# A two-layer LoRA and attention kernel on one core: unit 3's heads transposed on TensorE, the first matrix in three pieces, layer 0's results turned by blocks and an exchange

## The chip, the cores and the metric

The kernel runs on one NeuronCore of a Trainium2 chip. The core has a matrix engine (TensorE, PE in the profile; its weight loads are PEld), a vector engine (VectorE, DVE), a scalar engine (ScalarE, ACT), a general engine (GpSimd, POOL), and a sequencer that mostly issues transfers (SyncE, SP). 16 DMA engines move data between HBM and the on-chip memory. Each engine runs its own list of instructions in order and waits on semaphores for the others.

The metric is the device time of the whole kernel in microseconds. Before the change it is 1206.94 us, the median of three runs (1206.44 to 1207.21).

## What is computed

Eight sequences (B = 8) of 128 rows by 512 columns, all in float32, go through two layers. Each layer adds its result to its input.

```python
# layer 0, per sequence b
c   = x[b] @ weight[adapter_ids[b]].T               # 512 x 512, an adapter's own matrix
w   = softmax over the best 2 of 8 gates (c @ gate_w.T)
x1  = x[b] + c @ base_w.T + base_b + 2 * sum_e w[e] * (c @ A[e].T) @ B[e].T
# layer 1, per sequence b
q, k, v = x1 @ Wq.T, x1 @ Wk.T, x1 @ Wv.T           # 32 query heads, 8 key heads of 128
q, k    = rope(rmsnorm(q)), rope(rmsnorm(k))
o       = attention(q over 512 cached rows from 16 pages, plus the 128 own rows)
y       = o @ Wo.T
out     = x1 + 2 * (gates of 64 small experts * (y @ A_w.T)) @ B_w.T
```

## The kernel before

**Order of the work.** The order is written out by hand for all five engines: each engine's instructions run in the order in which the code emits them. Data dependences are kept by semaphores; a tile that reuses a buffer waits for the last reader of the buffer's former tile.

**Layer 0** is a loop of eight steps, `t = 0..7`. TensorE at step t does: `l0_adapter(t)` in two halves (the adapter's matrix times `x`, 16 products in 32 matmul instructions), between them `l0_turn_low(t - 1)` (a transpose of the gated low-rank values), then `l0_turn(t - 2)`, then `l0_experts(t - 1)` (L686, which completes the layer's result), then `l0_base(t)` (gates and base matrix, L640 and L645). From step 4 on pieces of layer 1 for units 0 and 1 stand in between: `project_whole` (L295), `norms`, `rotate`, `transpose_qk` and, at steps 6 and 7, the scores of unit 0.

`l0_experts(b)` makes the result `x1` on VectorE (L688), stores it to HBM, finds a power of two that brings it to range, and scales it on ScalarE into the buffer `xb` (L696). Layer 1's projections need that result with columns across the partitions. `l0_turn(b)` does this: four transposes of 128 by 128 on TensorE (L705) into a PSUM bank, and a copy by ScalarE (L707) into a half of `xo`. `xo` has four pairs of sequences with seven places each; places 0 to 3 hold the two results of a pair, 4 to 6 later hold sums.

Ahead of the loop TensorE runs `WARM` = 20 transposes of the identity matrix (L727). The first adapter matrix comes in two transfers of 512 KB, the others in one of 1 MB. SP issues these loads (`l0_load`), the loads of `x` (`l0_load_x`; three `xb` buffers, so the load for b + 3 waits until `l0_turn(b)` has read the buffer), the gathers of key pages and the stores of results, all in one queue. POOL issues the loads of projection weights (`load_q`).

**Layer 1** works in 64 units: a unit is one of the eight key heads of one sequence, with its four query heads. `iteration(u)` does, for unit u, four scores (`scores`, L436 for the cached keys and L439 for the own rows) into the two alternating PSUM banks `s0` and `s1`, masking with the smallest value taken along (`mask_exp`, VectorE L449), the exponential (ScalarE L460), the division by the sum (POOL L466), and for earlier units the values (`values(u - 2)`, L953) and the output projection.

The probabilities must be transposed before the values. This is done in two steps: VectorE transposes blocks of 32 by 32 into the tile `pb` (`blocks`, L471), and an exchange through HBM moves the blocks across partitions: `exchange_out(u)` writes `pb` to `px` with four transfers (L483, two each by SP and ScalarE's queue), `exchange_in(u)` reads it back as `pT` in the next iteration (L933). There is one `pb` buffer.

The rotated heads of unit u + 2 (four query heads and the key head) ride in the same exchange: `blocks_qk(u + 2, u)` transposes them by blocks into the rear columns of `pb` (L422), `exchange_in` reads them back as `qkb` (L930), and `heads_qk` copies them to `qkT` on ScalarE (L940). This holds for units 3 to 63. The heads of units 0, 1 and 2 are transposed on TensorE by `transpose_qk` (L361) and copied from PSUM (L366). Unit 0's `pb` lies in a free part of the weight tile `wo_t`.

At the end of the kernel six of the last layer's gated rows are transposed in a similar way by helpers that the change uses too: `turn_blocks` (VectorE, L372), `turn_out` (four writes to HBM, L380), `turn_in` (one read, L387), `turn_chunks` (a ScalarE copy that puts the blocks in order, L393).

`homes` is a tile of five places for the attention's outputs; the first is written by `evict_o(0)` in iteration 3.

Of the kernel before, what the change touches and what calls it, by code (L numbers as in the profile page):

```python
# [16 lines left out]
P = 128  # L17
B = 8
S = 128
DM = 512  # L20
# [18 lines left out]
SCALE = D ** -0.5  # L39
E1, R1, RD = 64, 8, 16  # L40
SC1 = 2.0
WARM = 20
TINY = 2.0 ** -60
EXPONENT = 0x7F800000
BIG = 3.0e38
# [13 lines left out]
def adaln_ffn_kernel(  # L59
# [98 lines left out]
    def sums_q(eng, g, *tees):  # L158

        w = wq_t[g]  # L160
        for t in tees:
            to, x, y = {3: (5, 3, 1), 2: (4, 5, 0), 4: (6, 2, 4), 1: (1, 1, 0)}[t]
            eng.tensor_tensor(w[:, to], w[:, x], w[:, y], ALU.add if t == 2 else ALU.subtract)  # L163
# [207 lines left out]
    def turn_blocks(rows, room):  # L371
        nc.vector.transpose(  # L372
            room.rearrange("p (k c a) -> p c k a", k=QD, c=NC),
            rows.rearrange("p (c k a) -> p c k a", c=NC, k=QD),
        )
# [10 lines left out]
    def turn_in(m, room):  # L386
        nc.sync.dma_start(  # L387
            out=room.rearrange("p (i f) -> p i f", i=QD), in_=m.rearrange("k b i f -> (k b) i f")
        )

    def turn_chunks(out, room):

        nc.scalar.copy(  # L393
            out.rearrange("p c (i a) -> p c i a", a=32),
            room.rearrange("p (i c a) -> p c i a", i=QD, c=NC),
        )
# [15 lines left out]
    def new_pb(u):  # L412

        if u == 0:
            home = wo_t[:, :4].rearrange("p x n -> p (x n)")[:, : QD * PW]
            pb_t[u] = home.rearrange("p (i f) -> p i f", i=QD)
            return
        pb_t[u] = wk1.tile([P, QD, XW], F32, tag="pb", name=f"pb_{u}")

# [56 lines left out]
    def exchange_out(u):  # L476

        pb = pb_t.pop(u)
        m = dram_x.tile([QD, 32, QD, XW], F32, tag="px", name=f"px_{u}")
        w = XW if u + 2 in range(3, NU) else PW  # L480
        for i in range(QD):
            eng = nc.sync if i < QD // 2 else nc.scalar
            eng.dma_start(  # L483
                out=m[:, :, i, :w].rearrange("k b f -> b k f"),
                in_=pb[i * 32 : (i + 1) * 32, :, :w],
            )
        px_t[u] = m


    with ExitStack() as l0:  # L490
# [6 lines left out]
        def l0_load(b):  # L497
            xT = p2.tile([P, NC, S], F32, tag="xT", name=f"xT_{b}", bufs=3)
            eng = nc.scalar if b == 0 else nc.sync
            eng.dma_start(out=xT.rearrange("p c n -> p (c n)"), in_=xt[b])  # L500
            wt = wt_home.pop(b)
            a = nc.sync.value_load(ids[0:1, b : b + 1])
            at = range(0, DM + 1, 2 * P if b == 0 else DM)
            for n, end in zip(at, at[1:]):
                nc.sync.dma_start(
                    out=wt.rearrange("p o n -> p (o n)")[:, NC * n : NC * end],
                    in_=w0[ds(a, 1), :, NC * n : NC * end].rearrange("e p n -> p (e n)"),
                )
            loaded[b] = [xT, wt]

        def l0_load_x(b):
            xb = p2.tile([P, DM], F32, tag="xb", name=f"xb_{b}", bufs=3)
            nc.sync.dma_start(out=xb, in_=x[b])
            loaded[b].append(xb)
# [169 lines left out]
        def l0_experts(b):  # L684
# [13 lines left out]
            nc.gpsimd.tensor_scalar(eps[:, b : b + 1], s, s, EPS, ALU.mult, ALU.mult)  # L698
            state[b] = xb

        def l0_turn(b):
            x1 = state.pop(b)
            tp = bank("o" if b >= B - 2 else "q", f"x1tp_{b}")
            for c in range(NC):
                nc.tensor.transpose(tp[:, c * S : (c + 1) * S], x1[:, c * P : (c + 1) * P], ident)  # L705
            half = xo[:, b // 2, b % 2 * 2 : b % 2 * 2 + 2]
            nc.scalar.copy(half.rearrange("p x c s -> p (x c s)"), tp[:, :DM])  # L707
# [20 lines left out]
        for t in range(B):  # L728
            l0_adapter(t, True)
            if t >= 1:  # L730
                l0_turn_low(t - 1)
            if t == 7:
                scores(0, 1, 1)
                mask_exp(0, 1)
                normalize(0, 0)
            l0_adapter(t, False)
            if t == 0:
                l0_fold()
            if t + 3 < B:
                l0_load(t + 3)  # L740
            if t + 2 < B:
                l0_load_x(t + 2)
            if t in (3, 4):
                load_q(t - 3)
            if 2 <= t <= 5:
                gather(0, (t - 2) * 4, (t - 1) * 4)
            elif t > 5:
                gather(1, (t - 6) * 8, (t - 5) * 8)
            if t >= 2:
                l0_turn(t - 2)  # L750
            if t == 4:
                project_whole(0, 0, 0, 1)
            if t == 5:
                norms(0)
                make_mask(0)
                project_whole(0, 1, 0, 1)
            if t == 6:
                transpose_qk(0)
                project_whole(0, 0, 1, 1)
            if t == 7:  # L760
                make_tables(2)
                norms(2)
                project_whole(0, 1, 1, 1)
                transpose_qk(1)
            if t >= 1:
                l0_experts(t - 1)
            if t == 7:
                scores(0, 2, 1)
                mask_exp(0, 2)
                normalize(0, 1)  # L770
                new_pb(0)
                blocks(0, 0)
            l0_base(t)
            if t == 0:
                l0_small()
            if t == 1:
                l0_rows()
                nc.vector.tensor_scalar_mul(nw[:, 0, :], nw[:, 0, :], -SCALE)
            if 1 <= t <= 4:
                l0_angles(t - 1)  # L780
            if t in (3, 6):
                gather_v(t // 3 - 1, 0, LC)
            if t in (4, 5):
                make_tables(t - 4)
            if t == 4:
                project_whole(0, 0, 0, 0)
            if t == 5:
                project_whole(0, 1, 0, 0)
                norms(1)
                rotate(0)  # L790
                sums_q(nc.gpsimd, 0, 3, 2)
            if t == 6:
                scores(0, 0, 1)
                mask_exp(0, 0)
                project_whole(0, 0, 1, 0)
                rotate(1)
                sums_q(nc.gpsimd, 0, 4)
            if t == 7:
                scores(0, 3, 1)
                mask_exp(0, 3)  # L800
                normalize(0, 2)
                blocks(0, 1)
                project_whole(0, 1, 1, 0, "kv")
# [8 lines left out]
        blocks(0, 2)  # L812
        blocks(0, 3)
        exchange_out(0)
        l0_turn(B - 2)
        l0_experts(B - 1)
        scores(1, 1)
# [104 lines left out]
    with ExitStack() as l1:  # L922
# [2 lines left out]

        def exchange_in(u):
            m = px_t.pop(u).rearrange("k b i f -> (k b) i f")
            if u + 2 in range(3, NU):
                qkb = wk1.tile([P, QD, NH * 32], F32, tag="qkb", name=f"qkb_{u + 2}")
                nc.sync.dma_start(out=qkb, in_=m[:, :, PW:])  # L930
                qkb_t[u + 2] = qkb
            pT = wk1.tile([P, QD, PW], F32, tag=f"pT{u % 2}", name=f"pT_{u}")
            nc.sync.dma_start(out=pT, in_=m[:, :, :PW])  # L933
            pT_t[u] = pT
# [325 lines left out]
        def iteration(u):  # L1260
# [48 lines left out]
            for h in range(REP):  # L1309
                if on(u):  # L1310
                    if (u, h) not in ((1, 0), (1, 1), (2, 0)):
                        scores(u, h)
                        mask_exp(u, h)
                    if h > 0 and (u, h) != (1, 1):
                        normalize(u, h - 1)

                    sums_o(u, h)
                    sums_w(u, h)
                    if 16 <= u < NU - 8 and (r, h) == (2, 3):
                        load_o(u // 16, (1, B12))  # L1320

                    if h == 2:
                        new_pb(u)
                        if u + 2 in range(3, NU):
                            blocks_qk(u + 2, u)
                    if h > 1:
                        blocks(u, h - 2)
                    if h == 1 and u == NU - 5:
                        f_fold()
                    if h == 3:  # L1330
                        z_blocks(u - NU + 4)
                    if h == (1 if u == NU - 3 else 2) and fb is not None:
                        yT_t[fb] = f_turn(fb, *f)
                if on(u - 3):
                    output(u - 3, h)
                    sums_a(u - 3, h)
                if h > 0 and slots:
                    project(k, j, slots[h - 1 : h])

                if (u, h) in WHOLE:  # L1340
                    project_whole(1, *WHOLE[u, h])
            if on(u - 3):
                add_output(u - 3, False)
            if on(u + 1) and (u + 1) % GH == 0:
                make_mask(units[u + 1][0])
            if u + 1 in range(3, NU):
                heads_qk(u + 1)

            if u < NU - 8:
# [202 lines left out]
```

## Time and profile before

| | |
|---|---|
| median of three runs | 1206.94 us (1206.44 to 1207.21) |
| the profiled execution | 1206.82 us |
| its span, first to last instruction | 1205.1 us |
| TensorE matmul busy | 1193.9 us, 99% |
| VectorE, POOL, ScalarE busy | 913.4, 741.0, 504.1 us |
| moved by DMA | 302.97 MB, mean 251 GB/s |
| layer 0's loop | from 6.9 us to about 109 us of the span |
| unit 3's first scores | at 145.81 us |

The busy shares are over the whole span. A matmul's duration overlaps with the next one's; what a group costs TensorE is the distance from its start to the next group's start. The timeline gives for each entry its start, its duration (or the sum of a merged group), the engine, the line, the operation, the tiles written and read, and in brackets the idle time before it with what ended it. The windows view gives the busy time of each engine in a stretch, the clock that TensorE was granted there (1.00 is full speed) and the DMA engines' share and rate. The chain of waits follows the work that ended last back through what released it.

### The profile page before, as it was taken

What the parts mean: (1) busy time and instruction counts of PE and PEld (TensorE: products, weight loads), DVE (VectorE), ACT (ScalarE), POOL (GpSimd) and SP (SyncE); (2) the same over time, 40 slices, a digit from 0 to 9 for tenths busy, and PEclk for the clock granted to TensorE, in tenths of its full rate; (3) what the DMA queues carried; (4) which work ended last, traced back from release to release, by engine and by line L of the source; (5) the groups of instructions that cost most, each with busy time, mean ns of one, the idle gap of its engine ahead of it and who ended that gap; (6) DMA issues with size and microseconds to landing.
All of it is one profiled execution on the core that took longest, in us unless ns stands there. A gap on an engine that the chain in (4) does not pass through costs nothing.

```text
span 1205.1 us, 16763 instructions
## 1 busy us (share of the span) xinstructions
PE 1193.9 (99%) x4147; PEld 716.3 (59%) x4147; DVE 913.4 (76%) x2104; ACT 504.1 (42%) x1457; POOL 741.0 (61%) x828
## 2 busy tenths in 40 slices
PE   9999999999999999999999999999999999999998
PEld 7666455565555556555556565555656565565554
DVE  2547788788888787878888887889887888887632
ACT  1345544444444443444444444444444444443211
POOL 3545769778755587578757685787657684643100
PEclk9999999999999999999999999999999999999999
DMA  8823787888878988898789878987889887897742
GB/s 317 290 85 113 243 249 237 266 279 274 264 253 256 304 242 262 270 297 290 246 252 289 292 230 283 299 287 246 270 256 298 256 262 246 270 286 228 234 137 99
DMA packets 205684, 302.97 MB, mean 251 GB/s; under 512 B 84755, under 2 KB 119828, under 8 KB 204564
## 3 DMA queue, kind: packets, MB, share of 16 engines
q1 hardware_dynamic: 170692, 197.30, 53.4%
q10 hardware_dynamic: 18576, 52.21, 13.6%
q0 software_dynamic: 16320, 52.40, 12.4%
q8 instruction: 33, 0.54, 0.2%
q14 instruction: 63, 0.52, 0.1%
HBM read 185.77 MB, written 116.06 MB: 250 GB/s over the span
## 4 chain that ended last, share of the span: by engine, by line
PE 89%; DMA 4%; DVE 2%; POOL 2%; issue 1%; SPq 1%; ACT 1%; ACTq 0%; DVEq 0%; POOLq 0%
PE o L953 20%; PE p L262 19%; PE s L436 17%; PE y L1078 13%; PE s L439 4%; PE p L295 3%; DMA px<-pb 3%; PE cp L623 2%; PE y L1091 2%; PE op L1439 2%; PE bp L645 2%; PE fr L863 1%; DVE pb L471 1%; PE fz L863 1%; DMA kt<-in_kc 1%
## 5 line engine op out<-in xcount | busy, mean ns | idle before, releaser
L460 ACT ACTIVATE p<-p,low 128x640 f32<-128x640 f32 x256 | 211.8, 827 | 432.8 <-DVE den L465 269.6
L466 POOL TENSOR_SCALAR p<-p,den 128x640 f32<-128x640 f32 x256 | 209.8, 820 | 228.3 <-DVE den L465 227.2
L449 DVE CUSTOM_DVE_ANT_0 p<-s,mask,rs 128x640 f32<-128x640 f32 x256 | 222.3, 879 | 80.8 <-PE s L439 80.2
L262 PE MATMUL p<-wqkv,xo 128*128 128x384 f32 x784 | 280.5, 486 | 0.0
L436 PE MATMUL s<-kt,qkT 128*128 128x512 f32 x504 | 258.2, 594 | 5.3 <-ACT qkT L940 2.9
L953 PE MATMUL o<-pT,vt 128*128 128x512 f32 x512 | 230.2, 592 | 0.0
L471 DVE STREAM_TRANSPOSE pb<-p 128x640 f32<-128x640 f32 x252 | 207.9, 826 | 19.9 <-POOL p L466 19.8
L1078 PE MATMUL y<-wo,oT 128*128 128x256 f32 x784 | 206.4, 380 | 0.0
L262 PEld LDWEIGHTS p<-wqkv,xo 128*128 128x128 f32 x784 | 148.5, 190 | 68.2 <-POOL wqkv L163 0.5
L439 PEld LDWEIGHTS s<-qkT 128*128 128x128 f32 x504 | 95.8, 190 | 120.5 <-issue 120.5
L203 POOL DMA_INDIRECT vt<-in_vc,vrow x128 | 138.5, 1082 | 41.7 <-issue 31.3
L953 PEld LDWEIGHTS o<-pT,vt 128*128 128x128 f32 x512 | 97.2, 190 | 107.9 <-issue 92.5
L436 PEld LDWEIGHTS s<-kt,qkT 128*128 128x128 f32 x504 | 94.7, 190 | 77.4 <-issue 28.9
L1078 PEld LDWEIGHTS y<-wo,oT 128*128 128x128 f32 x784 | 131.9, 191 | 8.6
L311 ACT ACTIVATE sq<-c 128x128 f32<-128x128 f32 x320 | 98.9, 309 | 9.5 <-DVE pb L471 1.4
L439 PE MATMUL s<-qkT 128*128 128x128 f32 x504 | 96.8, 274 | 0.0
L317 POOL TENSOR_TENSOR rs<-ss,mhalf 128x5 f32<-128x5 f32 x64 | 82.4, 1288 | 5.3
L976 ACT COPY oT<-o 128x512 f32<-128x512 f32 x64 | 37.4, 585 | 102.2 <-PE o L953 88.2
L315 POOL TENSOR_SCALAR ss<-ss,eps 128x5 f32<-128x5 f32 x64 | 27.5, 429 | 75.6 <-ACT sq L311 75.6
L422 DVE STREAM_TRANSPOSE pb<-ca 128x640 f32<-128x640 f32 x61 | 50.9, 834 | 19.8 <-DMA px<-pb 10.6
L953 PE MATMUL o<-pT,vn 128*128 128x512 f32 x128 | 65.4, 592 | 0.0
L265 DVE TENSOR_TENSOR c<-c,p 128x384 f32<-128x384 f32 x84 | 44.8, 534 | 24.2 <-PE p L262 23.9
(197 smaller groups left out, 1442.1 us busy)
## 6 DMA issues: line engine op xcount, KB each, us to landing
pT<-px SPq DMA_DIRECT2D x64, 1280.0 KB, 7.5
px<-pb SPq DMA_DIRECT2D x122, 400.0 KB, 5.5
px<-pb ACTq DMA_DIRECT2D x122, 400.0 KB, 5.5
qkb<-px SPq DMA_DIRECT2D x61, 320.0 KB, 3.5
kt<-in_kc SPq DMA_DIRECT2D x512, 32.0 KB, 4.7
wqkv<-in_wqkv POOLq DMA_DIRECT2D x32, 384.0 KB, 4.9
wo<-in_wo POOLq DMA_DIRECT2D x17, 512.0 KB, 7.6
yd<-yp POOLq DMA_DIRECT2D x12, 512.0 KB, 9.4
```

The source lines that it names most:

```text
L203: nc.gpsimd.indirect_dma_start(out=kv_t[step][1][:, c, :], out_offset=None, in_=vc, in_offset=bass.IndirectOffsetOnAxis(ap=vrow[:, hf, at ...
L262: nc.tensor.matmul(out=ps, lhsT=xo[:, pr, x, c, :], rhs=w[:, c, :], start=(c == 0), stop=(c == 1))
L311: nc.scalar.activation(sq, cs[:, at : at + D], AF.Square, accum_out=ss[:, h : h + 1])
L317: nc.gpsimd.tensor_tensor(rs, ss, mhalf, ALU.pow)
L436: nc.tensor.matmul(out=s[:, :L], lhsT=qkT[:, h, :], rhs=kt[:, :, g % GH, :], start=True, stop=True)
L439: nc.tensor.matmul(out=s[:, L:NK], lhsT=qkT[:, h, :], rhs=qkT[:, REP, :], start=True, stop=True)
L449: nc.vector.tensor_tensor_reduce(out=p, in0=s_t.pop((u, h))[:, :NK], in1=mask_t[st], scale=rs_t[u][:, h : h + 1], scalar=BIG, op0=ALU.add, ...
L460: nc.scalar.activation(p, p, AF.Exp, bias=low, scale=-1.0, accum_out=den)
L466: nc.gpsimd.tensor_scalar(p_t[u, h], p_t[u, h], den, 1.0, ALU.mult, ALU.mult)
L471: nc.vector.transpose(pb_t[u][:, :, h * w : (h + 1) * w].rearrange("p i (j a) -> p j i a", a=32), p_t.pop((u, h)).rearrange("p (j i a) -> ...
L953: nc.tensor.matmul(out=o, lhsT=vt[:, c, j * D : (j + 1) * D] if c < LC else vn_t.pop(u), rhs=pT[:, c], start=(c == 0), stop=(c == LC),)
L1078: nc.tensor.matmul(out=y_t["y"][:, half * HN : (half + 1) * HN], lhsT=part(key)[:, i * S : (i + 1) * S], rhs=wo_t[:, slot(w, key[0] // (B ...
```

## The change

- `WARM` becomes 24.
- The first adapter matrix comes in three transfers, of 256, 256 and 512 KB.
- The results 0 to 5 of layer 0 are no longer transposed on TensorE. At the end of step t (1 to 6) `l0_out(t - 1)` turns the result by blocks on VectorE into a room in `xo` and writes it to HBM with four transfers of SP; in the middle of the next step `l0_in` reads it back; at the step after that `turn_chunks` copies it into its half on ScalarE (for result 5 after the loop). Results 6 and 7 stay on TensorE. `l0_load_x(t + 2)` moves on SP's queue from ahead of the gathers to the end of the step, after `l0_out`.
- Unit 3's heads no longer ride in unit 1's exchange. `transpose_qk(3)` does them on TensorE in iteration 1, after the scores of head 2; it takes one turn of the two score banks. The exchange of unit 1 is that much smaller (320 instead of 400 KB a transfer).
- Unit 1's blocks go to the tile `homes` instead of the `pb` buffer.

```diff
-WARM = 20
+WARM = 24
...
+    def x1_room(b):
+        return xo[:, (0, 1, 3)[b % 3], 4:6].rearrange("p x c s -> p (x c s)")
+
+    def x1_half(b):
+        return xo[:, b // 2, b % 2 * 2 : b % 2 * 2 + 2].rearrange("p x c s -> p (x c) s")
...
         if u == 0:
             home = wo_t[:, :4].rearrange("p x n -> p (x n)")[:, : QD * PW]
             pb_t[u] = home.rearrange("p (i f) -> p i f", i=QD)
+            return
+        if u == 1:
+            pb_t[u] = homes.rearrange("p x n -> p (x n)").rearrange("p (i f) -> p i f", i=QD)
             return
...
-        w = XW if u + 2 in range(3, NU) else PW
+        w = XW if u + 2 in range(4, NU) else PW
...
-            at = range(0, DM + 1, 2 * P if b == 0 else DM)
+            at = (0, P, 2 * P, DM) if b == 0 else (0, DM)
...
+        def l0_out(b):
+            room = x1_room(b)
+            turn_blocks(state.pop(b), room)
+            x1m_t[b] = turn_out(f"x{b}", room)
+
+        def l0_in(b):
+            turn_in(x1m_t.pop(b), x1_room(b))
...
             if t + 3 < B:
                 l0_load(t + 3)
-            if t + 2 < B:
-                l0_load_x(t + 2)
...
-            if t >= 2:
-                l0_turn(t - 2)
             if t == 4:
                 project_whole(0, 0, 0, 1)
...
+            if t >= 3:
+                turn_chunks(x1_half(t - 3), x1_room(t - 3))
+            if t >= 2:
+                l0_in(t - 2)
             if t >= 1:
                 l0_experts(t - 1)
...
+            if 1 <= t < B - 1:
+                l0_out(t - 1)
+            if t + 2 < B:
+                l0_load_x(t + 2)
...
         exchange_out(0)
+        turn_chunks(x1_half(B - 3), x1_room(B - 3))
         l0_turn(B - 2)
...
-            if u + 2 in range(3, NU):
+            if u + 2 in range(4, NU):
                 qkb = wk1.tile([P, QD, NH * 32], F32, tag="qkb", name=f"qkb_{u + 2}")
...
+                    if (u, h) == (1, 2):
+                        transpose_qk(3)
+
                     sums_o(u, h)
...
-                        if u + 2 in range(3, NU):
+                        if u + 2 in range(4, NU):
                             blocks_qk(u + 2, u)
...
-            if u + 1 in range(3, NU):
+            if u + 1 in range(4, NU):
                 heads_qk(u + 1)
```

More of the change, by code (lines that the diff above doesn't have):

```diff
@@ L699, in l0_experts @@
             state[b] = xb
+        x1m_t = {}
+        def l0_out(b):
[4 more added lines that the diff above has]
+            turn_in(x1m_t.pop(b), x1_room(b))
         def l0_turn(b):
```

## The prediction

> **What bounds the kernel now.** I read the page's busy times first, then the gaps in TensorE's timeline, then the granted clock around the largest gap, then the chain of waits through it, and last the rows of operations that already do what the change adds.
>
> The page:
>
> ```profile
> PE 1193.9 (99%) x4147; PEld 716.3 (59%) x4147; DVE 913.4 (76%) x2104; ACT 504.1 (42%) x1457; POOL 741.0 (61%) x828
> ```
>
> TensorE is the bound: work taken from it counts, work moved to other engines counts only where TensorE then waits for it. Its timeline (start, duration, what, idle before it):
>
> ```profile
> 1.36 4.53 PE L727 MATMUL idle<-ident 128*128 128x128 f32 x20 [1.36 <-POOL ident masks.py:199]
> 6.92 5.60 PE L623 MATMUL cp<-xT,wqkv 128*128 128x128 f32 x32 [1.03 <-DMA wqkv<-in_w]
> ...
> 30.61 0.60 PE L705 MATMUL x1tp<-ident,xb 128*128 128x128 f32 x4
> 31.05 1.02 PE L686 MATMUL bp<-lb,lowT 128*128 128x512 f32 x2
> ...
> 98.51 0.71 PE L361 MATMUL tq<-ident,ca 128*128 128x128 f32 x5
> 99.05 1.02 PE L686 MATMUL bp<-lb,lowT 128*128 128x512 f32 x2
> ...
> 141.93 1.02 PE L953 MATMUL o<-pT,vn 128*128 128x512 f32 x2
> 145.81 1.12 PE L436 MATMUL s<-kt,qkT 128*128 128x512 f32 x2 [2.85 <-ACT qkT L940]
> ```
>
> Matmuls overlap, so a group's price is start to next start: four transposes of a layer-0 result 0.44 us (30.61 to 31.05), five head transposes 0.54 us (98.51 to 99.05). Only two idle stretches are over 1 us: 1.03 us ahead of the first real matmul, and 2.85 us ahead of unit 3's first scores. The second costs twice. Windows around it (length, busy and count for PE, PEld, DVE, ACT, POOL, then granted clock, DMA share, GB/s):
>
> ```profile
> 143.79:147.21 3.42, 1.40 (x5) 0.90 (x6) 3.00 (x8) 1.54 (x3) 2.41 (x3) 1.00 1.05 390
> 147.21:150.63 3.42, 3.42 (x7) 1.71 (x6) 3.38 (x6) 2.47 (x12) 3.09 (x4) 0.50 0.99 287
> 150.63:154.04 3.41, 3.41 (x12) 1.93 (x11) 2.43 (x6) 2.10 (x6) 2.40 (x4) 1.00 0.97 301
> ```
>
> After the stretch that holds the gap the clock is granted at 0.50 for 3.42 us. The chain says what made unit 3 late:
>
> ```profile
> 133.11 8.19 DMA px<-pb
> ...
> 141.52 0.84 DVE pb L422
> 142.37 0.74 DVE pb L471
> ...
> 143.23 0.88 DVE p L449
> ...
> 144.22 0.92 ACT p L460 x2
> 145.14 0.62 ACT qkT L940
> ```
>
> VectorE may not refill the one `pb` buffer before unit 1's exchange has left it; its later work, ScalarE's exponential and the copy of unit 3's heads all stand behind that.
>
> The pieces of the new layer-0 exchange run already, at the end, for the last layer's gated rows. By line, L380 is the turn's writes (ns), L387 its read-back, L372 VectorE's blocks; each second line is issue to landing:
>
> ```profile
> L380 SPq DMA_DIRECT2D yx<-xo x24: 302/448/1656, 1096.6 to 1158.7; - x24
> DMA to landing us min/median/max: 2.5/5.6/7.4
> ```
>
> ```profile
> L387 SPq DMA_DIRECT2D rooms<-yx x6: 338/369/651, 1116.7 to 1160.6; - x6
> DMA to landing us min/median/max: 2.7/2.8/6.3
> ```
>
> ```profile
> L372 DVE STREAM_TRANSPOSE xo<-rooms x6: 668/669/712, 1081.9 to 1155.4; 128x512 f32<-128x512 f32 x6
> ```
>
> **The start.** The first matmul waits for half of the first matrix, 512 KB, whose landing the chain of waits puts at 6.79 (issued at 2.64). In three pieces the first 256 KB land an estimated 0.6 us earlier (256 KB at the 406 GB/s of the window that follows). The warm-up's 20 transposes stand 0.213 us apart (their timeline row, less the last one's pipeline tail); 24 end at 6.55, which replaces the landing as the limit. So the start comes 0.37 us sooner. Those first matmuls are 0.213 us apart up to 10.68 and 0.112 us after it (32 of them take 5.60 us, later 16 take 1.95), so cold time is worth about half: **-0.2**. Bounds: 0, if the first piece lands no earlier; -1.8, if the closed idle stretch lets full speed come one 3.4 us stretch sooner. I take the small value because until 5.7 the warm-up alone had not brought it. The small end is also near what can be kept: VectorE at the second step waits until 28.95 for `nw`, whose transfer is tied to other loads, so its results for step 3 cannot come over 1.1 us earlier.
>
> [...]
>
> **Layer 0's results.** Six groups of four transposes go: 6 x 0.436 = **-2.61**. At steps 2 and 3 they also covered ScalarE's `cT` copy; at step 1, which has none, the next eight matmuls (L640) take 1.01 us against 0.93: **+0.16**. The copy out of PSUM (0.59) becomes one from SBUF (0.62 in the same end phase). VectorE gets 0.67 us at the end of steps 1 to 6; at steps 1 to 5 it otherwise idles 1 to 9 us waiting for L686, so that is hidden, without that cover it would delay `low` by 0.67 each. At step 6 it is not: block turning goes ahead of `mask_exp(0, 1)`, then come ScalarE's exponential, `cT`, the norms, and unit 1's head copy, for which TensorE already waited until 100.14. That chain gains 0.73 and loses a 0.48 copy: 0.25 later, and the 0.43 saved there is waited away: **+0.68** (from 0, if the chain has slack, to 1.1, if both engines' delays add).
>
> SP gets 24 writes of 0.45 us and 6 reads of 0.37 us, 13 us in all. They are put ahead of the next `x` load, which moves past the page gathers and the state's store. `x` 3 goes out at about 34 instead of 31.28 and is needed by POOL's addition at 43.94; matrix 5 goes at 36 instead of 33.55 and is needed at 60.10. Later SP is earlier than before, since it no longer waits for the transposes (40.62, 49.97, 64.45). POOL's queue has the same order, but its weight loads share the DMA engines with 3 MB more; weights for 49.72 landed at 44.55, those for 64.22 at 59.64: hidden.
>
> What is added as a wait is ScalarE's `turn_chunks`. At step 3 result 0 is turned on VectorE at 31.9, written by 34 and landed at 39; the read goes out after the gathers at 40 and lands at 42.7 by the median, 43.5 behind matrix 5. Queued behind it on ScalarE are the scaling of result 2 and `ex`, then VectorE's `low` 3, for which TensorE comes at about 46.4 (47.39 less the gains): I estimate **+0.2**. Bounds: 0 at a landing by 43.3, +3 at the longest read (6.3 us, so 46.3). At the later steps the data is there microseconds before ScalarE. Result 5 is turned after the loop, ahead of the copy at 116.67, before which ScalarE idles 0.76 us: 0.62 fits.
>
> **Unit 3.** Five transposes are added at unit 1: **+0.54**; ScalarE's copy 0.69 replaces one of 0.71, VectorE loses 0.83. Unit 1's blocks go to the still free `homes`, so unit 2's blocks start at 137.4, not 141.52; its last scores are masked at 139, its exchange leaves near 144 instead of 147.14. Heads for unit 3 are ready 17 us early. Late next would be the score bank (freed by 137), then unit 4's heads: landed near 155, needed near 160. So the gap goes, **-2.85**, and with it half of a 3.42 us stretch, **-1.71** (eight projection matmuls took 4.44 instead of 2.74). Bounds: 0, if another wait stands there; -4.56.
>
> [...]
>
> **Sum:** -0.2 - 2.61 + 0.16 + 0.68 + 0.2 + 0.54 - 2.85 - 1.71 = -5.8 us. The profiled execution took 1206.82 (span 1205.1 and 1.7 around it) and becomes 1201.0; the median, 0.12 above it, goes from 1206.94 to 1201.1.
>
> **Rivals.**
> - *Layer 0 gives its gain back* (14%). Read 0 lands at 46.3, or the weights for 64.22 come late. For: the transfers run at 363 to 365 GB/s between 50 and 60, and 3 MB come on top. Against: those weights have 4.6 us of slack, 2.2 after the shift. +3: 1204.1.
> - *The gap stays or moves* (8%): something else holds unit 3 or 4. Against: every later supplier is some 4 us ahead. Half kept 1203.4 (half of 4.56 back), all kept 1205.7.
> - *The gap goes but the clock falls there anyway* (4%). For: that stretch of 3.42 us held 41% busy time; a new short wait may do the same. 1202.8.
> - *Full clock sooner* (6%). For: the idle 1.03 us goes. Against: the `nw` bound above. The whole 1.8 instead of 0.2: 1199.5.
> - *Slower* (8%): ScalarE's wait at step 3. Each microsecond that result 0 lands after 43.3 is one of TensorE's; from about 2.8 us on the clock falls too, +1.7. The gain is gone when it lands at 47.4 (5.8 less 1.7 is 4.1 us late); a landing at 49.8 costs 8.2 in all and gives 1209.4. For: nothing else is queued ahead on ScalarE that could hide it. Against: the longest rows, 7.4 for a write and 6.3 for a read, together make 47.7, which is 1207.2.
>
> **Numbers.** The forecast has 60%, its own range 1199.9 to 1202.4. A change under 0.2%, 2.4 us, can hardly be told from none. Fully kept gaps (4%), the far part of the first rival (4%) and the near part of the slow one (3%) end inside that; the rest of the slow one (5%) is beyond it. Low and high take in early clock and a lost layer 0: 1199.0 to 1204.6. Faster 0.84, same 0.11, slower 0.05.
>
> **What would show it.** The 24 x1tp transposes gone; first matmul at 6.55; no 2.85 gap, granted clock 1.00 through 140 to 150; scores of unit 3 at 141.7 instead of 145.81 (the sum without the clock); from the next unit on the timeline shifted by a constant 5.8. Wrong if TensorE shows new idle time at 46, at 98 or ahead of unit 4.

## The result and the profile after

The changed kernel takes 1212.82 us, the median of 18 executions (1207.90 to 1219.28), against 1206.9 us for the kernel before beside it (1204.97 to 1210.17). The ratio is 1.0048 with a 95% interval of 1.0035 to 1.0060: it is slower by some 5.8 us, where 5.8 us less was forecast. Single executions of one kernel lie up to 12 us apart, so every comparison below is given with its interval.

The profiled execution took 1212.4 us, its span is 1210.6 us. The page's busy times:

```profile
PE 1191.4 (98%) x4132; PEld 711.9 (59%) x4132; DVE 915.7 (76%) x2109; ACT 504.4 (42%) x1457; POOL 737.2 (61%) x828
```

TensorE is busy for 2.5 us less than before (24 transposes fewer, five more for unit 3, four more ahead of the loop, and 3.42 us at half clock before, at 147.21, which the changed kernel does not have), and the span is 5.5 us longer. So its idle time grew by 8 us. Where it is, TensorE's timeline of the changed kernel says (start, duration, what, and in brackets the idle time before it with what ended it). First the start:

```profile
1.36 4.71 PE L746 MATMUL idle<-ident 128*128 128x128 f32 x24 [1.36 <-POOL ident masks.py:199]
5.91 1.08 PE L632 MATMUL cp<-xT,wqkv 128*128 128x128 f32 x8
7.32 1.16 PE L632 MATMUL cp<-xT,wqkv 128*128 128x128 f32 x8 [0.32 <-DMA wqkv<-in_w]
10.30 2.05 PE L632 MATMUL cp<-xT,wqkv 128*128 128x128 f32 x16 [1.83 <-DMA wqkv<-in_w]
```

The first matmul comes a whole microsecond earlier than before (5.91 against 6.92), and its first 8 matmuls take 1.08 us, the pace of later (16 take 1.95). But then the second piece is 0.32 us late and the third 1.83 us.

Step 4 of layer 0, in the same view:

```profile
45.81 1.95 PE L632 MATMUL cp<-xT,wt 128*128 128x128 f32 x16
51.53 0.33 PE L689 MATMUL ltp<-ident,low 128*128 128x128 f32 x1 [3.77 <-DVE low L677]
```

The transpose of `low` 3, the place where the prediction had put 0.2 us, waits 3.77 us. The chain of waits through it (start, length, what):

```profile
40.71 8.11 DMA xo<-yx_x
...
49.36 0.72 ACT xb L705
50.08 0.20 ACT ex L668
...
51.19 0.30 DVE low L677
...
51.53 0.33 PE ltp L689
```

The read of result 0 is issued at 40.71 and takes 8.11 us. ScalarE's copy out of it (L399) starts at 48.84 after 7.54 us of waiting, and the scaling of result 2 and the exponential of step 3's gates are queued behind it. Why the read takes so long is seen in SP's queue (start, issue time, what), in which everything stands behind four writes:

```profile
23.31 0.33 SPq L698 DMA_DIRECT2D x1d<-x  x1
33.62 1.84 SPq L380 DMA_DIRECT2D yx_x<-xo  x4
35.55 0.40 SPq L522 DMA_DIRECT2D xb<-in_x  x1
...
36.94 0.34 SPq L514 DMA_DIRECT2D wo<-in_w  x1
...
40.71 0.48 SPq L387 DMA_DIRECT2D xo<-yx_x  x1
```

SP issues nothing from 23.7 to 33.62: the writes wait for VectorE's block turning of result 0 (32.88), which stands on VectorE behind `nw`'s landing at 30.73. The load of matrix 5, which runs below that send it first issue at 29.7 to 31.5, waits with them until 36.94. In windows of the changed kernel (granted clock, DMA share and GB/s are the last three columns):

```profile
30.00:35.00 5.00, 5.00 (x23) 2.87 (x22) 4.06 (x11) 0.59 (x1) 0.00 (x0) 1.00 0.12 36
...
40.00:45.00 5.00, 5.00 (x23) 2.87 (x22) 4.16 (x15) 0.59 (x1) 1.35 (x3) 1.00 1.01 359
45.00:50.00 5.00, 2.76 (x19) 2.09 (x17) 0.29 (x1) 1.16 (x3) 3.91 (x5) 1.00 1.00 312
```

and of the kernel before:

```profile
30.00:35.00 5.00, 5.00 (x27) 3.32 (x27) 3.60 (x14) 1.81 (x4) 0.65 (x2) 1.00 0.59 168
...
40.00:45.00 5.00, 5.00 (x22) 3.02 (x21) 3.11 (x13) 2.05 (x4) 1.32 (x2) 1.00 0.73 238
```

The DMA engines are mostly idle between 30 and 35 (0.12 instead of 0.59), and full from 40 to 50 (1.01 and 1.00), where the read, which takes some 2.8 us at the end of the kernel, is under way for 8. The clock stays at 1.00 through the wait.

Last, step 7 and units 3 and 4, TensorE's timeline after:

```profile
103.42 1.13 PE L445 MATMUL s<-kt,qkT 128*128 128x512 f32 x2 [0.67 <-ACT qkT L366]
...
146.57 1.02 PE L445 MATMUL s<-kt,qkT 128*128 128x512 f32 x2
...
165.94 1.10 PE L445 MATMUL s<-kt,qkT 128*128 128x512 f32 x2 [1.54 <-DMA kt<-in_kc]
```

Unit 3's scores (146.57) follow without a gap, as forecast. Twenty microseconds later unit 4's wait 1.54 us for their pages of keys.

The shift of the two profiles against each other, at the first scores of units 0, 2, 4 and 62: +3.1, +3.8, +1.7, +5.5 us. So layer 0 and the start cost 3 us where 2 were to be won, and unit 3's part gives 2. The last 3.7 us come after unit 13, spread over 900 us (single waits of 0.2 to 1.1 us make 4.8 us there, 2.3 before); the kernel before, profiled a second time below, moves against its own first profile by nearly as much (-1.4 at unit 4, -2.8 at unit 36, +0.4 at unit 62), so nothing is read from them. This pair of profiles therefore places only 1.7 us of the loss; the rest of the account goes by the medians of the runs below.

### The profile page after: what moved, and what is told of

Its sections match the earlier page's. It is cut to its first block, busy times and chain, and to the rows that moved or that the text cites. A ratio compares the mean times of both kernels' runs of the same rounds, so it can differ in the third digit from the quotient of the medians.

```text
span 1210.6 us, 16777 instructions
## 1 busy us (share of the span) xinstructions
PE 1191.4 (98%) x4132; PEld 711.9 (59%) x4132; DVE 915.7 (76%) x2109; ACT 504.4 (42%) x1457; POOL 737.2 (61%) x828
## 4 chain that ended last, share of the span: by engine, by line
PE 86%; DMA 4%; POOL 3%; issue 2%; SPq 2%; DVE 1%; ACT 1%; ACTq 0%; POOLq 0%
PE o L977 20%; PE p L262 18%; PE s L445 16%; PE y L1102 13%; PE s L448 4%; PE p L295 3%; PE y L1115 2%; PE op L1466 2%; PE bp L654 2%; DMA px<-pb 2%; PE cp L632 2%; PE fr L887 1%; PE fz L887 1%; POOL p L475 1%; DMA kt<-in_kc 1%
## 5 line engine op out<-in xcount | busy, mean ns | idle before, releaser
L480 DVE STREAM_TRANSPOSE pb<-p 128x640 f32<-128x640 f32 x248 | 204.7, 826 | 22.5 <-POOL p L475 22.5
L315 POOL TENSOR_SCALAR ss<-ss,eps 128x5 f32<-128x5 f32 x64 | 24.0, 375 | 63.8 <-ACT sq L311 63.8
```

Of the source, the lines that this page charges most:

```text
L480: nc.vector.transpose(pb_t[u][:, :, h * w : (h + 1) * w].rearrange("p i (j a) -> p j i a", a=32), p_t.pop((u, h)).rearrange("p (j i a) -> ...
```

## The experiments

Theory A, from the trace: the loss is made in layer 0, by ScalarE's copy of the chunks standing ahead of work that TensorE needs, while SP, held by VectorE's blocks, leaves the DMA engines idle and then overfills them. Theory B: the start's pieces make it. Theory C: unit 3's part is worth less than its gap, since another supplier is next. The first four runs take the three parts of the change apart, each alone on the kernel before or taken out of the changed kernel.

### Unit 3's part alone

```diff
 (on the kernel before)
+        if u == 1:
+            pb_t[u] = homes.rearrange("p x n -> p (x n)").rearrange("p (i f) -> p i f", i=QD)
+            return
...
+                    if (u, h) == (1, 2):
+                        transpose_qk(3)
...
-            if u + 1 in range(3, NU):
+            if u + 1 in range(4, NU):
                 heads_qk(u + 1)
```

> The kernel before with unit 3's part alone (heads of unit 3 transposed on TensorE, unit 1's blocks in homes). The theory that layer 0's exchange alone makes the change slower: the 2.85 us gap ahead of unit 3 and the 3.4 us at half clock go, 0.54 us of transposes come, so 3 to 4.5 us faster than before (1202.5 to 1204). The rival that this part moves the waits into the later units (the changed profile has 1.5 us for a page ahead of unit 4 and some 3.7 us more idle time from unit 13 on): no gain or a loss, 1206 to 1209.

Measured: 1206.21 us, ratio 0.9999 (0.9984 to 1.0014). The gap is gone, and TensorE's timeline shows what was next:

```profile
154.46 1.56 PE L262 MATMUL p<-wqkv,xo 128*128 128x384 f32 x4 [0.69 <-DVE c L265]
...
161.11 1.10 PE L445 MATMUL s<-kt,qkT 128*128 128x512 f32 x2 [0.81 <-DMA kt<-in_kc]
```

Of the 4 us net that the forecast gave to this part the median shows none (the interval is -1.9 to +1.7 us). Theory C holds in so far as the part is worth less than its gap. That the waits above are made by the part is not shown: five of the nine profiles without it also wait ahead of unit 4's scores, for 0.3 to 1.1 us. How much is left is worked out below from all the profiles.

### The exchange in layer 0 alone

```diff
 (on the kernel before: the changed kernel's layer 0, its old start and unit 3)
-            if t >= 2:
-                l0_turn(t - 2)
...
+            if t >= 3:
+                turn_chunks(x1_half(t - 3), x1_room(t - 3))
+            if t >= 2:
+                l0_in(t - 2)
...
+            if 1 <= t < B - 1:
+                l0_out(t - 1)
+            if t + 2 < B:
+                l0_load_x(t + 2)
```

> The kernel before with layer 0's exchange alone (results 0 to 5 by blocks, loads of x moved). The exchange theory: TensorE waits for low 3 at step 4 for about 4 us, the gap at unit 3 stays, so 7 to 11 us slower than before (1214 to 1218). The rival that the start or unit 3's part makes the loss: the exchange by itself within 2 us of before, or faster by its 2.6 us of transposes.

Measured: 1212.29 us, ratio 1.0058 (1.0034 to 1.0082): alone it costs as much as the whole change. ScalarE's timeline at step 3, then TensorE's:

```profile
50.01 0.62 ACT L399 COPY xo<-xo 128x512 f32<-128x512 f32 x1 [9.89 <-DMA xo<-yx_x]
...
52.68 0.47 PE L686 MATMUL ltp<-ident,low 128*128 128x128 f32 x1 [6.10 <-DVE low L674]
```

and the window behind it, at half the clock (third column from the end):

```profile
50.45:57.28 6.83, 4.60 (x19) 4.29 (x20) 2.66 (x8) 1.85 (x5) 1.68 (x3) 0.50 0.99 329
```

The read took 9.5 us here. TensorE loses 6.10 us of waiting and up to 3.4 more (half of 6.83 us) to the clock, against 2.6 us of transposes saved.

### The start alone

```diff
 (on the kernel before)
-WARM = 20
+WARM = 24
...
-            at = range(0, DM + 1, 2 * P if b == 0 else DM)
+            at = (0, P, 2 * P, DM) if b == 0 else (0, DM)
```

> The kernel before with the start alone (24 warm-up transposes, first matrix in three pieces). The exchange theory: within 1 us of before. The rival that the three pieces hurt (the changed profile has 0.32 and 1.83 us of waits for the second and third piece, and nw lands at 30.73 instead of 28.95): 1 to 4 us slower. If the warm-up counts for the clock: up to 1.8 us faster.

Measured: 1209.63 us, ratio 1.0032 (1.0012 to 1.0051). The start does not save 0.2 us, it costs some 3 (3.9 by the ratio). TensorE waits for the third piece, and the clock falls to half for 6.83 us from 11.90 (its timeline, then a window):

```profile
10.72 2.73 PE L629 MATMUL cp<-xT,wqkv 128*128 128x128 f32 x16 [2.46 <-DMA wqkv<-in_w]
```

```profile
11.90:18.73 6.83, 6.83 (x26) 5.68 (x26) 1.34 (x8) 0.89 (x2) 0.58 (x1) 0.50 1.03 407
```

### The changed kernel with the old start

```diff
 (on the changed kernel)
-WARM = 24
+WARM = 20
...
-            at = (0, P, 2 * P, DM) if b == 0 else (0, DM)
+            at = range(0, DM + 1, 2 * P if b == 0 else DM)
```

> The change without its start (20 transposes, two pieces), so exchange and unit 3 together. The exchange theory: within 1.5 us of the changed kernel, 1211 to 1214. The rival that the start makes the loss: 1205 to 1209.

Measured: 1210.56 us, ratio 1.0031 (1.0014 to 1.0049), 2 us below the whole change. The three parts alone come to 7.0, -0.1 and 3.9 us by their ratios, 10.8 in all, and the whole to 5.8. Why it is less than the sum was not shown. Two things are seen in the profiles. The wait for `low` 3 is 5.45 us here (in an execution of 1217.54 us, the slowest of the twelve) and 3.77 with the new start: the data is there 1.1 us later here (ScalarE's copy at 49.97 for 48.84), and TensorE comes 0.6 us earlier. And the start alone lost clock behind its wait (the next 8 matmuls, of L735, take 1.97 us), which the changed kernel did not (1.10, L738).

### Which order in the exchange costs

Three runs on the exchange alone, all with the old start and the old unit 3. In the first, ScalarE's copy goes behind the exponential of the gates, at the end of the step; SP's order stays.

```diff
 (on the exchange alone)
-            if t >= 3:
-                turn_chunks(x1_half(t - 3), x1_room(t - 3))
             if t >= 2:
                 l0_in(t - 2)
...
+            if t >= 3:
+                turn_chunks(x1_half(t - 3), x1_room(t - 3))
             if 1 <= t < B - 1:
                 l0_out(t - 1)
```

> The exchange alone, with turn_chunks put at the end of the step, behind the gate's exponential on ScalarE. Theory: the loss is ScalarE's in-order wait for the read; then TensorE no longer waits for low 3 (4 to 6 us of idle time plus up to 3.4 us of clock go), at most 1 to 2 us of waiting for result 0 itself are left ahead of step 4's projection: about 7 us faster than the exchange alone, 1204 to 1207. Rival: SP, held by VectorE's blocks, sends the weight matrices and projection weights late; then the wait moves to the projection at step 4 and the time stays above 1210.

In the second ScalarE's order stays, and SP's four writes and the load of `x` are sent behind the next step's load of a matrix, so that nothing ready waits for VectorE. `l0_blocks` is the block turning, taken out of `l0_out`.

```diff
 (on the exchange alone)
             if t + 3 < B:
                 l0_load(t + 3)
+            if t >= 2:
+                l0_out(t - 2)
+            if 2 <= t and t + 1 < B:
+                l0_load_x(t + 1)
...
             if 1 <= t < B - 1:
-                l0_out(t - 1)
-            if t + 2 < B:
-                l0_load_x(t + 2)
+                l0_blocks(t - 1)
+            if t == 0:
+                l0_load_x(2)
```

> The exchange alone, with its four writes and the load of x sent after the next step's matrix, so that SP does not hold that matrix back for VectorE. turn_chunks stays where it was. Theory that SP's hold makes the read late: between 30 and 35 us the DMA engines are busy over 0.5 instead of 0.27, the read of result 0 lands 3 us or more sooner and the wait for low 3 falls from 6.1 to under 3 us: 1206 to 1209. Theory that only ScalarE's order counts: the wait stays at 4 to 6 us, 1211 to 1213.

The third has both edits.

```diff
 (on the exchange alone: the two diffs above together)
+            if t >= 2:
+                l0_out(t - 2)
...
+            if t >= 3:
+                turn_chunks(x1_half(t - 3), x1_room(t - 3))
             if 1 <= t < B - 1:
                 l0_blocks(t - 1)
```

> Both of these edits together. If both mechanisms are real, this is the fastest of the three: all of TensorE's idle time from 30 to 70 us gone, 24 transposes saved less 0.8 us: 1203 to 1206. If the added 3 MB of transfers are the cause by themselves, still 2 us or more of waits in layer 0, for weights or matrices, and no gain over before.

| | median us | ratio to before (95%) | wait for `low` 3, us | DMA share 30 to 35 |
|---|---|---|---|---|
| exchange alone | 1212.29 | 1.0058 (1.0034 to 1.0082) | 6.10 | 0.27 |
| copy late | 1206.30 | 1.0002 (0.9985 to 1.0019) | none | 0.17 |
| writes late | 1207.42 | 1.0003 (0.9988 to 1.0019) | 1.69 | 0.90 |
| both late | 1206.99 | 1.0005 (0.9991 to 1.0020) | none | 0.98 |

With the copy late, ScalarE still waits for the read, but with nothing of TensorE's behind it (ScalarE's timeline):

```profile
45.40 0.30 ACT L665 ACTIVATE ex<-lg,nv 128x8 f32<-128x8 f32 x1
49.15 0.62 ACT L399 COPY xo<-xo 128x512 f32<-128x512 f32 x1 [3.45 <-DMA xo<-yx_x]
```

The exponential, for which TensorE's transpose waits by way of VectorE, is done 3.45 us before the copy starts. With the writes late, the hole in the transfers is filled, the read, issued at 39.0, lands at 45.7, and the wait shrinks to 1.69 us. All four also wait for `low` 2 a step earlier (1.23, 2.01, 1.40 and 1.23 us); the second profile of the kernel before has 1.01 us there. Behind the 2.01 us, with the copy late, the clock is at half for 3.41 us (the granted clock is 0.84 from 35 to 40 and 0.81 from 40 to 45).

So either edit takes away the loss that can be measured: it needs both the early copy and a read that lands late. The hole in the transfers costs nothing by itself (copy late: 0.17, and no loss). Nor is it what makes the read long, as theory A had it. With both edits the share between 30 and 35 is 0.98, and the read still takes 8.9 us (SP's queue, then ScalarE's timeline):

```profile
38.22 0.37 SPq L387 DMA_DIRECT2D xo<-yx_x  x1
```

```profile
47.13 0.62 ACT L399 COPY xo<-xo 128x512 f32<-128x512 f32 x1 [3.72 <-DMA xo<-yx_x]
```

In the four kernels that send the writes late (these two and the two at the end) it takes 6.7 to 8.9 us, in the four with the changed kernel's order 8.1 to 9.5, and from 40 to 45 the DMA share is 0.91 or more in all eight. On average the data is there 3.2 us sooner with the writes late: 2.2 because the read is issued sooner, 1.0 because it is shorter. What the three runs do not show is the forecast's gain. With both edits and the early clock the first scores of unit 2 come at 126.8 us, against 128.5 in the second profile of the kernel before, 1.7 us earlier, where the forecast's terms for layer 0 without the wait make 1.8 (2.61 less 0.16 and 0.68). That is one pair of profiles. The median is not lower: an interval of -1.1 to +2.4 us holds neither that gain nor its absence for sure.

### The kernel before a second time

> The kernel before, unchanged, profiled a second time: whether the 2.85 us gap ahead of unit 3, the stretch at half clock after it and the full clock at 10.7 us are there in every execution. If the forecast's reading was typical: a gap of 2.5 to 3.2 us, a stretch at 0.50 after it, full clock at 9 to 12. If it was one case of several: full clock near 5 and no stretch at half clock.

The code is the one before, without an edit. One execution, 1207.25 us. Its start and its gap, TensorE's timeline:

```profile
6.75 4.00 PE L623 MATMUL cp<-xT,wqkv 128*128 128x128 f32 x32 [0.91 <-DMA wqkv<-in_w]
...
144.49 1.13 PE L436 MATMUL s<-kt,qkT 128*128 128x512 f32 x2 [2.08 <-ACT qkT L940]
```

The 32 matmuls that took 5.60 us in the first profile take 4.00 here (16 take 1.95 later in the first profile). So the half speed up to 10.68 that the prediction reckoned with was one execution's, and the gap is 2.08 us, not 2.85.

### Pieces or warm-ups

```diff
 (on the kernel before: the pieces alone)
-            at = range(0, DM + 1, 2 * P if b == 0 else DM)
+            at = (0, P, 2 * P, DM) if b == 0 else (0, DM)
```

> Before, with the first matrix in three pieces and the 20 warm-up transposes as they were. Theory (the pieces cost the start its 3 us): a wait of 1 to 2.5 us on TensorE for the third piece at 10 to 11 us, which lands at 10.0 to 10.9 where the second of two lands at 8.1 to 9.4; the median 2 to 3.5 us above before's. Rival (the four more warm-ups did it, or the pieces only together with them): a wait under 0.5 us and the median within 0.8 us of before's.

```diff
 (on the kernel before: the warm-ups alone)
-WARM = 20
+WARM = 24
```

> Before, with 24 warm-up transposes instead of 20 and the two pieces as they were. Theory (the pieces cost the 3 us): the median within 1 us of before's, with the second piece landed before TensorE asks for it. Rival (the warm-ups did it): 2 to 3.5 us above before's.

Measured: the pieces alone 1208.41 us, ratio 1.0007 (0.9993 to 1.0020); the warm-ups alone 1206.53 us, 0.9995 (0.9982 to 1.0008). TensorE's timeline with the pieces:

```profile
1.36 3.86 PE L727 MATMUL idle<-ident 128*128 128x128 f32 x20 [1.36 <-POOL ident masks.py:199]
6.35 2.15 PE L623 MATMUL cp<-xT,wqkv 128*128 128x128 f32 x16 [1.12 <-DMA wqkv<-in_w]
9.92 2.05 PE L623 MATMUL cp<-xT,wqkv 128*128 128x128 f32 x16 [1.42 <-DMA wqkv<-in_w]
11.90 1.10 PE L719 MATMUL rk<-wo 16*128 16x64 f32 x8
```

and with the warm-ups:

```profile
6.91 3.96 PE L623 MATMUL cp<-xT,wqkv 128*128 128x128 f32 x32 [0.17 <-DMA wqkv<-in_w]
10.80 1.10 PE L719 MATMUL rk<-wo 16*128 16x64 f32 x8
```

A window of each, pieces first, warm-ups second (last two columns: DMA share, GB/s):

```profile
3.00:12.00 9.00, 6.46 (x47) 5.88 (x45) 0.00 (x0) 0.00 (x0) 0.56 (x2) 1.00 0.88 305
```

```profile
3.00:12.00 9.00, 8.83 (x59) 8.27 (x58) 0.06 (x1) 0.58 (x1) 0.55 (x2) 1.00 0.90 337
```

The pieces make the wait: in all three profiles with three pieces TensorE goes on with the last at 9.92 to 10.72 us, 1.42 to 2.46 us after it wants it, and the transfers run at 305 to 312 GB/s from 3 to 12 us. With two pieces they run at 330 to 339 in three profiles (the first of before, the warm-ups alone, the version below without what was found), and TensorE does not wait for the second piece there. With the pieces the first matrix is done 1.1 us later (11.90 against 10.80), though it was begun 0.56 us sooner. That the pieces alone cost time is not shown: 1.5 us by the medians, 0.8 by the ratio, not the 2 to 3.5 expected, and the interval is -0.8 to +2.4. In the run of both, the 2.46 us wait was followed by half clock for 6.83 us; in the pieces alone the 1.42 us was not (the next 8 matmuls take 1.10 us, 1.97 in the run of both). Whether that is what both together cost beyond the two alone was not settled.

### A version of the change without what was found

```diff
 (on the changed kernel: the old start, writes late, copy late; unit 3's part stays)
-WARM = 24
+WARM = 20
...
+            if t >= 2:
+                l0_out(t - 2)
...
-            if t >= 3:
-                turn_chunks(x1_half(t - 3), x1_room(t - 3))
             if t >= 2:
                 l0_in(t - 2)
...
+            if t >= 3:
+                turn_chunks(x1_half(t - 3), x1_room(t - 3))
             if 1 <= t < B - 1:
-                l0_out(t - 1)
+                l0_blocks(t - 1)
...
```

> The changed kernel without its start, with result t turned by blocks at a step's end but its four writes and the load of x sent behind the next step's load of a matrix, and the chunks copied at the end of the step; unit 3's part is in it. Theory (of the changed kernel's losses only these two orders and the three pieces count, and unit 3's part is worth what its gap was less its transposes and the wait for pages, 0.5 to 1.2 us): 1205.5 to 1206.8, and no wait over 2 us on TensorE in the first 60 us. Rival (any change of a few us ahead is given back at the next supplier): within 0.3 us of before's, with waits for the pages of unit 4 of 1.5 us or more.

Measured: 1204.67 us, ratio 0.9982 (0.9967 to 0.9997), 0.18% faster than before (0.03 to 0.33%) and, ratio over ratio, 0.66% faster than the changed kernel. The median lies 0.8 us under the range that was expected. ScalarE's and TensorE's timelines at step 4:

```profile
45.24 0.62 ACT L399 COPY xo<-xo 128x512 f32<-128x512 f32 x1 [1.58 <-DMA xo<-yx_x]
```

```profile
46.63 0.27 PE L689 MATMUL ltp<-ident,low 128*128 128x128 f32 x1
```

No wait in the first 60 us but the 0.93 us for the first half matrix. Unit 4's scores come 4.4 us before those of the first profile of before; a wait of 0.97 us is left ahead of them. The run with both edits late differs from this one in unit 3's part alone; ratio against ratio the part is worth 2.8 us here, where alone it showed 0.1. Each ratio is known to 0.15% (1.8 us) either way, so the medians do not settle its worth.

### The pages of unit 4 earlier

```diff
 (on the version above)
             first, end = ((0, 8), (8, NPP))[u % GH]
+            if u == 2:
+                end = NPP
+            if u == 3:
+                first = end
             if pages:
-                gather(st + 1, first, first + 5)
+                gather(st + 1, first, min(first + 5, end))
```

> As the run before, and all 16 pages of units 4 and 5 asked for in iteration 2, none in iteration 3. Theory (the pages of unit 4 are what ends the gain of unit 3's part): the wait of 0.8 to 1.5 us ahead of unit 4's scores is gone and the median 0.5 to 1.2 us under that of the run before. Rival (the pages only move the traffic: in iteration 2 they stand ahead of the reads of unit 1's or behind those of unit 2's block-turned data): a wait of about the same length for that data, and no difference over 0.4 us.

Measured: 1210.44 us, ratio 1.0022 (1.0010 to 1.0033), 5.8 us above the run before it. SP's queue, then TensorE:

```profile
141.96 11.02 SPq L193 DMA_DIRECT2D kt<-in_kc  x11
153.08 0.85 SPq L492 DMA_DIRECT2D px<-pb  x2
158.58 0.54 SPq L959 DMA_DIRECT2D qkb<-px  x1
```

```profile
160.79 2.93 PE L262 MATMUL p<-wqkv,xo 128*128 128x384 f32 x4 [5.58 <-DVE c L265]
```

Eleven pages in a row hold SP's queue for 11.02 us, and SP's two writes of unit 2's exchange leave at 153.08 (at 142.50 in the version above). They land at 158.53, only then may VectorE refill the one `pb` buffer, and behind that stands its copy `c`, for which TensorE waits 5.58 us and then has half its clock (0.51 granted from 159.1 to 165.9). The rival is right in kind, a wait for block-turned data, at a far higher price than it was given. It is the loss of layer 0 once more: the eleven pages put ahead in SP's queue held back the two writes, which were needed, by 10.6 us.

## Why the prediction was wrong, step by step

**The wait for `low` 3 at step 4 (+0.2, bounds 0 and +3): the step that failed.** The mechanism and the place were named, and the times of the issues were right to within two microseconds (blocks at 32.9 for 31.9, `x` 3 at 35.6 for 34, the read at 40.7 for 40). The term that failed is the read's length: 2.7 us by the median and 6.3 at most, from the rows at the end of the kernel, where six such reads were seen. Between 1116 and 1161 us, where those rows come from, the DMA share is 0.65; at 40 to 50 us of the changed kernel it is 1.00, and the read takes 8.1, 9.5 in the exchange alone. So a transfer's price was taken from one load and used at another. The prediction moved the loads of `x` 3 and matrix 5 behind the blocks and only asked whether these loads would still be in time (they are), not what traffic the read would meet. With the writes late the read takes 6.7 to 8.9 us too, so the hole that SP's silence leaves explains little of the length; which transfers make it long stays open. That the data would be there microseconds before ScalarE at the later steps was wrong as well: in the changed kernel ScalarE waits 6.33 and 0.91 us for the next two reads, with no wait of TensorE behind them.

Of the 11.6 us between the 5.8 forecast and the 5.8 measured the other way, this term makes some 6 by the medians (exchange alone against copy late), the start some 2 (the changed kernel with the old start) and unit 3's part the most of the rest; the parts do not add up exactly.

**The rival "slower" (8%)** is what happened. Its threshold holds roughly: result 0 was there at 48.8, 5.5 us after 43.3, and TensorE waited 3.8, since it came 1.4 us later than forecast itself. Its case against, that the longest rows make 47.7, failed with the same prices. The 3.77 us cost no clock as well (1.00 granted from 45 to 55). The rival had reckoned with that cost from about 2.8 us on, from the one gap of 2.85 us; no run shows such a bound: half clock came behind gaps of 2.0 and 2.08 us and not behind these 3.77.

**The start (-0.2, bounds 0 and -1.8).** The first piece and the first matmul came as forecast or earlier (5.91 for 6.55). What was left out is the last piece: in three pieces the same 1 MB comes more slowly (305 to 312 GB/s from 3 to 12 us, 330 to 339 in two), and TensorE, which now starts earlier and faster (8 matmuls in 1.08 us), runs into it. That sign, a loss, lay outside the bounds. The half speed up to 10.68 us, from which "the warm-up alone had not brought it" was concluded, was a case: behind 20 warm-ups and nothing else, the first 32 matmuls take 5.60 and 5.54 us in the first profile of before and in the version without what was found, but 4.00 and 3.83 in the second profile of before and with both edits late.

**Layer 0's results (-2.61, +0.16, +0.68).** The 0.68 was right: at step 7 TensorE waits 0.67 us (0.66 in the version without what was found) for the copy of unit 1's heads, ahead of unit 0's scores of head 2. The sum agrees in one pair of profiles: with the wait for `low` 3 away unit 2's scores come 1.7 us earlier for a forecast 1.8. No median shows it.

**Unit 3 (+0.54, -2.85, -1.71).** The gap goes, in all five profiles that have the part. But 2.85 us was the largest of the gaps: the nine profiles without the part have 1.83 to 2.85. Half clock follows in some (0.50 granted for 3.41 to 3.42 us in both profiles of the kernel before and with the writes late), not in all (1.00 from 141 to 151.5 with the copy late, behind a gap of 2.20). And "every later supplier is some 4 us ahead" was wrong: with the part unit 4's scores waited 0.8 to 1.5 us in all four profiles (three times for their pages; the early pages left out), without it 0.3 to 1.1 us in five of nine. From the first scores of unit 2 to those of unit 4 it takes 34.4 us in the mean of the nine, 32.5 in the mean of the four: 1.9 us, less 0.54 for the transposes, 1.3 net where 4.0 were forecast.

**What would make it wrong** was named: new idle time at 46, at 98, or ahead of unit 4. All three came (3.77, 0.67 and 1.54 us); the second is the one that the sum had with 0.68.

## What to carry to other kernels

Price a transfer by a row from a stretch with the DMA load that it will meet (the read took 2.8 us where the DMA share was 0.65 and 8.1 where it was 1.00), and when a queue is made to wait for an engine, ask not only whether what stands behind comes in time, but how much later everything behind it is issued and what waits for that. A copy that waits for a transfer goes behind the work that the bounding engine needs, not ahead of it; in the exchange alone that one line was worth 6 us, more than the 2.6 us of the 24 transposes that the change saved. A gap and a clock step seen in one profile are one case: profile the kernel twice before a term of a sum rests on them.

## What the runs showed of the hardware that was not expected

- A wait of TensorE was followed by half clock in some places and not in others, and not by its length: the 3.77 us in the changed kernel cost no clock; the 2.0 us ahead of unit 3 in the run with the writes late were followed by 3.42 us at 0.50. The windows view, of the changed kernel and then of that run (length, then PE's busy time; the clock is the third column from the end):

```profile
46.21:49.62 3.41, 1.55 (x14) 1.36 (x13) 0.00 (x0) 0.78 (x2) 2.48 (x4) 1.00 0.98 325
49.62:53.04 3.42, 1.50 (x14) 1.51 (x14) 2.57 (x8) 0.92 (x3) 3.42 (x6) 1.00 1.00 331
```

```profile
143.06:146.47 3.41, 1.43 (x5) 0.90 (x6) 3.00 (x8) 1.53 (x3) 2.44 (x3) 1.00 1.06 389
146.47:149.89 3.42, 3.42 (x7) 1.74 (x6) 3.38 (x6) 2.50 (x12) 3.09 (x4) 0.50 1.02 298
```

  Ahead of unit 3, a gap of 2.08 us in the second profile of the kernel before was followed by 0.50 from 145.60 to 149.01, and one of 2.20 us with the copy late was not (1.00 from 141 to 151.5). The half-clock stretches in the windows views are 3.41 to 3.42 us long, 6.83 in the start alone and the exchange alone. What decides whether a wait costs clock was not shown.
- Transposes alone were enough to bring TensorE to its later pace in some profiles. In the run with the pieces alone the 20 warm-ups take 3.86 us and the 16 matmuls behind them 2.15 (16 take 1.95 later in the first profile of before); in the first profile of before the 20 warm-ups take 4.53 and the 32 behind them 5.60, in the second the 32 take 4.00. Why it differs from run to run was not shown.
